# Cross-attention on one core: the rest of the context loaded in blocks and turned by VectorE, Wv turned into a tile of its own, and the last keys' products in 32-column tiles

## The chip, the cores and the metric

The kernel runs on one core of a Trainium2 chip. The metric is the device time in microseconds of one execution; before the change the median of three runs is 282.15 us (280.95 to 282.51). All arithmetic is in 32-bit floats.

## The reference

```
Q = x @ Wq                      # x: 16 x 256 x 256, 8 heads of 256
K = ctx @ Wk;  V = ctx @ Wv     # ctx: 16 x 77 x 192
score = Q K^T / sqrt(256)       # masked keys at -inf
attn  = softmax(score)
out   = (attn V) @ Wo + x
out   = layernorm(out) * gamma + beta
```

## The kernel before, in words

The kernel never forms Q, K and V. For each head h it forms G_h = Wk_h Wq_h^T (192 x 256), so that scores are x (G_h^T ctx^T), and U_h = Wv_h Wo_h (192 x 256), so that the output of a head is attn (ctx U_h). The 192 rows of G and U are kept as 128 (tiles gA, uA) and 64 (gB, uB); the context, transposed, likewise: cA holds the first 128 of its 192 features for all 16 x 77 keys, and cB the last 64, twice, in both halves of the partitions, so that products of depth 64 can run two at a time, one in each half of the rows of TensorE's array. Heads are worked in places: pair a holds heads a and a + 4.

The order on every engine is written out by hand: instructions run in each engine's queue in the order of the source, and waits between engines come from the tiles they share. PSUM has eight banks, all of one ring ("mm", pool `ps_mm`), so the ninth tile waits until the first has been copied out. SyncE issues every load, in the order of the source; load number n also waits until load n - 8 has landed.

The stages, in order:

- Loads: parts of Wk and Wq in rows, the first 336 keys of the context in rows (`load_c(0, first)`, tile c_sb, with `first` = 3 groups of 112 rows), the other halves of Wk and Wq in blocks of 32 rows (`load_blocks`), the other 896 keys (`load_c(first, NCR)`), Wv in blocks (16 loads of 96 KB), Wo (4 of 512 KB), the mask as integers into the tile bias, and x of the first four batches in blocks (`load_xT`, 4 loads of 256 KB in pieces of 256 bytes). Later, in the order of the source: x in rows, gamma, beta, then x of the next batches.
- TensorE turns the row-loaded weights and context by transposes (`turn_q`, `turn_k`, `turn_c`), VectorE turns the block-loaded ones 32 x 32 at a time (`turn_blk`, `turn_v`, `transpose_x`).
- `g_of`, `rest_of_g` and `of_pair` form G; `a_of_places` forms a = G^T ctx^T of the first four batches.
- `turn_c(first, NCR)` turns the rest of the context with TensorE (L653). The copies out of PSUM alternate between ScalarE and VectorE (`evacuate`), and GpSimd makes cB's second copy (L664), then cRA and cRB, the last 13 keys of each batch (L780, L781), zeroes vr (L782) and turns the integer mask into bias (L786).
- `of_pair` with Wv and Wo forms uA (tile pu, L676), `rest_of_pairs` forms uB (tile pw, L690), which GpSimd copies to the other half of the partitions (L805). GpSimd then forms differences of the blocks of uA and uB (part t2, L808 and L809), and adds to bias the not-a-number of a batch whose keys are all masked (L814).
- `prepare_last` forms vr, the values of the last 13 keys of all batches: eight PSUM tiles pr, each of 32 output columns for both halves e; `part_A` (L274) of depth 128 and `part_B` (L284) of depth 64. vr is laid out in blocks of 32 columns, of which 26 hold values; the other 6 are zeros. VectorE turns it during the loop (`turn_last`).
- The loop over 16 batches: scores (L313), softmax on VectorE (L328, L335, L348), ScalarE (L342) and GpSimd (L356), values of the next batch (pv, L241 and L252), a of the next four batches (pa, L199 and L213), attention times values (pm and po, L429; po, L378), the sum with x and the layer norm.

In the weights of `of_pair`, pgb reads contiguous columns of kT_blk, while pu reads every fourth column of wvT:

```python
def wv_part(a, e, n):
    return flat(wvT[half(e), a]).rearrange("p (l n) -> p n l", n=4)[:, n]
```

Of the kernel before, what the change touches and what calls it, by code (L numbers as in the profile page):

```python
# [8 lines left out]
F32 = mybir.dt.float32  # L9
I32 = mybir.dt.int32  # L10
AF = mybir.ActivationFunctionType
ALU = mybir.AluOpType
# [3 lines left out]
P = 128  # L16
H = 8
D = 256
EPS = 1e-05
GB = 4  # L20
KM = 64
# [32 lines left out]
def kernel(  # L54
# [15 lines left out]
    S2, DL = c.shape[1], c.shape[2]  # L70
    LB = DL - P
    CR = 112
    NCR = B * S2 // CR
    NG = B // GB
    QT = S // P
    NT = B * QT
# [5 lines left out]
    NL = DL // BK  # L82
    PW = (NF + 1) * BK
    assert KM == 2 * BK and NM == NF and 2 * KR <= BK
    assert NCR * CR == B * S2 and NG * GB == B and DI == 2 * P and D == 2 * P and 2 * LB == P


    engines = mybir.EngineType
# [25 lines left out]
    def of_e(u, e):  # L114
        return u[:, 3 - 2 * e : 5 - 2 * e].rearrange("p q n i c -> p (q n) i c")
# [3 lines left out]
    cB = const.tile([P, B, S2], F32, tag="cB", name="cB")  # L119
    cRA = const.tile([P, B, KR], F32, tag="cRA", name="cRA")  # L120
    cRB = const.tile([P, B, KR], F32, tag="cRB", name="cRB")
    vr = const.tile([P, B, DI], F32, tag="vr", name="vr")
    p_ring = [const.tile([P, NM, PW], F32, tag=f"p{i}", name=f"p_{i}") for i in range(2)]
    for p in p_ring:
        nc.gpsimd.memset(p[:, :, 2 * S2 :], 0.0)
# [10 lines left out]
    def flat(ap):  # L136
        return ap.rearrange("p a b -> p (a b)")

    def half(i):
        return slice(i * LB, (i + 1) * LB)  # L140
# [31 lines left out]
    def transpose_x(g, j):  # L172

        cols = xT_of[g][:, j * NM : (j + 2) * NM]
        nc.vector.transpose(cols, cols)
# [91 lines left out]
    def prepare_last():  # L267


        pr = [ps_mm.tile([P, 2, B, KR], F32, tag="mm", name=f"pr_{n}") for n in range(DI // BK)]  # L270

        def part_A(e):
            for n, o in enumerate(pr):
                nc.tensor.matmul(  # L274
                    o[:, e].rearrange("p b k -> p (b k)"),
                    flat(of_e(uA, e)[:, n]),
                    flat(cRA),
                    start=(e == 0),
                    stop=(e == 1),
                )  # L280

        def part_B(e):
            for n, o in enumerate(pr):
                nc.tensor.matmul(  # L284
                    o[:, e].rearrange("p b k -> p (b k)"),
                    flat(of_e(uB, e)[half(n % 2), n]),
                    flat(cRB[half(n % 2)]),
                    start=(e == 1),
                    stop=(e == 0),
                )  # L290

        part_A(0)
        part_B(0)
        part_B(1)
        part_A(1)
        for n, o in enumerate(pr):
            to = vr[:, :, n * BK : n * BK + 2 * KR]
            evacuate(to.rearrange("p b (e k) -> p e b k", e=2), o)
# [241 lines left out]
    early = ctx.enter_context(tc.tile_pool(name="early", bufs=1))  # L540
    pools[0] = turned = early
    with tc.tile_pool(name="wonce", bufs=1) as wp:
        c_sb = wp.tile([CR, NCR, DL], F32, tag="c", name="c_sb")


        wq_nat = wp.tile([P, 2, 2, 2 * D], F32, tag="w128", name="wq_nat")
# [13 lines left out]
            for i in range(NM):  # L560
                nc.sync.dma_start(to[i * BK : (i + 1) * BK], blocks[i])

        def load_c(lo, hi):
            nc.sync.dma_start(c_sb[:, lo:hi, :], c_rows[:, lo:hi, :])

        first = -(-GB * S2 // CR)
        nc.sync.dma_start(wk_nat[:, 0], wk_rows[0][:, : 2 * D])
        nc.sync.dma_start(wq_nat[:, 0], wq_rows[0][:, :, : 2 * D])
        nc.sync.dma_start(wk_nat[:, 1], wk_rows[1][:, : 2 * D])
        nc.sync.dma_start(wq_nat[:, 1], wq_rows[1][:, :, : 2 * D])  # L570
        nc.sync.dma_start(wk_last, wk_ends[:, : 2 * D])
        load_c(0, first)
        for e in range(2):
            load_blocks(wk_blk[:, e], wk_blocks[2 * e + 1])
            load_blocks(wq_blk[:, e], wq_blocks[2 * e + 1])
        load_c(first, NCR)

        warm = const.tile([P, 1], F32, tag="warm", name="warm")
        nc.scalar.activation(warm, eps, AF.Exp)
# [8 lines left out]
            load_blocks(wvT[:, a], wv_blocks[a])  # L588
        for a in range(NF):
            nc.sync.dma_start(wo_of[a // 2][:, a % 2], wo_rows[a])  # L590
        nc.sync.dma_start(
            bias_f.bitcast(I32), mask.rearrange("b k -> (b k)").partition_broadcast(P)
        )
# [24 lines left out]
        def turn_q(e, u):  # L618
            chunks = [
                wq_nat[:, e, t, u * D + dc * P : u * D + (dc + 1) * P]  # L620
                for dc in range(2) for t in range(2)
            ]
            pt = turn_chunks(chunks, f"q_{e}_{u}")
            evacuate(flat(qT[:, e, u]), flat(pt))

        def turn_k(e):
            pt = turn_chunks([wk_nat[:, e, n * P : (n + 1) * P] for n in range(4)], f"k_{e}")
            evacuate(
                kT[:, e].rearrange("p u n l -> p (u n) l")[:, :, :P], pt
            )  # L630
# [13 lines left out]
                    blk[:, e].rearrange("p m (n c) -> p m n c", c=BK),  # L644
                )

        def turn_c(lo, hi):
            for r in range(lo, hi, 2):
                n = min(2, hi - r)
                pc = ps_mm.tile([P, 4, P], F32, tag="mm", name=f"pc_{r}")  # L650
                for lc in range(2):
                    for j in range(n):
                        nc.tensor.transpose(  # L653
                            pc[:, 2 * lc + j, :CR],
                            c_sb[:, r + j, lc * LB : lc * LB + P],
                            ident[:CR, :CR],
                        )
                rows = slice(r * CR, (r + n) * CR)
                evacuate(flat(cA)[:, rows].rearrange("p (j m) -> p j m", m=CR), pc[:, :n, :CR])
                evacuate(  # L660
                    flat(cB)[LB:, rows].rearrange("p (j m) -> p j m", m=CR),
                    pc[LB:, 2 : 2 + n, :CR],
                )
                nc.gpsimd.tensor_copy(flat(cB)[:LB, rows], flat(cB)[LB:, rows])  # L664

        def turn_v(a):
            blocks = wvT[:, a].rearrange("p m (c n) -> p m n c", n=4)
            nc.vector.transpose(blocks, blocks)

        def of_pair(out, a, weight, moving):

            for n in range(4):
                for e in range(2):
                    nc.tensor.matmul(  # L676
                        out[e][:, a % 2, :],
                        weight(a, e, n)[:, :P],
                        moving(a, e, n),
                        start=(n == 0),  # L680
                        stop=(n == 3),
                    )
# [23 lines left out]
            return kT_blk[half(e), a, n]  # L706

        def wv_part(a, e, n):
            return flat(wvT[half(e), a]).rearrange("p (l n) -> p n l", n=4)[:, n]

        def wo_part(a, e, n):
            return wo_of[a // 2][half(e), a % 2, n, :]
# [1 line left out]
        def g_of(e):  # L714

            pg = ps_mm.tile([P, 2, DI], F32, tag="mm", name=f"pg_{e}")
            for u in range(2):
                for dc in range(2):
                    nc.tensor.matmul(
                        pg[:, u],  # L720
                        kT[:, e, u, dc, :P],
                        qT[:, e, u, dc],
                        start=(dc == 0),
                        stop=(dc == 1),
                    )
            nc.scalar.mul(gA[:, NF * e : NF * e + 2], pg, D ** -0.5)
# [23 lines left out]
        keep_busy(4)  # L750
        turn_q(0, 0)
        turn_q(0, 1)
        turn_k(1)
        g_of(0)
        turn_q(1, 0)
        turn_q(1, 1)
        turn_k_last()
        turn_c(0, first)
        g_of(1)
        rest_of_g(0)  # L760
        rest_of_g(1)
# [14 lines left out]
        nc.sync.dma_start(bet, beta.partition_broadcast(P))  # L776
        a_of_places((2, 3))
        turn_v(3)
        turn_c(first, NCR)
        nc.gpsimd.tensor_copy(cRA, cA[:, :, KM:])  # L780
        nc.gpsimd.tensor_copy(cRB, cB[:, :, KM:])  # L781
        nc.gpsimd.memset(vr, 0.0)  # L782

        nc.gpsimd.tensor_scalar(bias_f, bias_f.bitcast(I32), 0.0, -MASKED, ALU.is_equal, ALU.mult)  # L786

        for j in range(NF // 2):
            pu = two_banks("pu", j)
            for a in range(2 * j, 2 * j + 2):  # L790
                of_pair(pu, a, wv_part, wo_part)
            for e in range(2):
                evacuate(
                    of_e(uA, e)[:, :, 2 * j : 2 * j + 2].rearrange("p n a c -> p a n c"),
                    pu[e].rearrange("p a (n c) -> p a n c", c=BK),
                )
        for j in range(NF // 2):
            for e, pw in enumerate(
                rest_of_pairs(j, (2 * j, 2 * j + 1), wv_part, wo_part, "pw")
            ):  # L800
                for i, engine in enumerate((nc.scalar.copy, nc.vector.tensor_copy)):
                    a = 2 * j + i
                    here, there = (of_e(uB, e)[half(k), :, a] for k in (i, 1 - i))
                    engine(here, pw[half(i)].rearrange("p (n c) -> p n c", c=BK))
                    nc.gpsimd.tensor_copy(there, here)  # L805
        for u in (uA, uB):
            t2, _, b22, b11, b12 = (u[:, q].rearrange("p n i c -> p (n i c)") for q in range(5))
            nc.gpsimd.tensor_tensor(t2, b22, b12, ALU.subtract)  # L808
            nc.gpsimd.tensor_tensor(t2, t2, b11, ALU.add)  # L809
        nan = wp.tile([P, B, 1], F32, tag="nan", name="nan")  # L810
        nc.vector.tensor_reduce(nan[:, :, 0], bias, AX.X, ALU.max)
        nc.gpsimd.tensor_tensor(nan, nan, nan, ALU.mult)
        nc.gpsimd.tensor_tensor(nan, nan, nan, ALU.subtract)
        nc.gpsimd.tensor_tensor(bias, bias, nan.to_broadcast([P, B, S2]), ALU.add)  # L814

        for j in range(0, GT, 2):
            transpose_x(0, j)
        prepare_last()


# [126 lines left out]
```

## Time and profile before

| What | us |
|---|---|
| median of three runs | 282.15 (280.95 to 282.51) |
| the profiled execution | 280.93 |
| its span, first to last instruction | 279.2 |
| PE busy in the span | 269.7 (97%) |
| DVE, ACT, POOL busy | 206.0, 166.4, 168.2 |
| one round of the loop | 14.1 |

The page lists busy time of each engine, then the span in slices, then the chain of work that ended last, then groups of instructions by line. PE is TensorE's products, PEld its weight loads, DVE VectorE, ACT ScalarE, POOL GpSimd, SP SyncE, SPq its queue of DMA issues. A group names its line, engine, output and input tiles, shapes and count. Two instructions of the profile make one 32-bit product of TensorE, so the 8 products of one part_A appear as 16.

The granted TensorE clock is 0.993 over the span, and lower only at its end.

### The profile page before, as it was taken

To read this page: it belongs to the slowest core of one execution; us is meant where nothing else is said; L and a number is where in the kernel's file an instruction comes from. 1 tells how busy PE (TensorE), PEld (TensorE's weight loads), DVE (VectorE), ACT (ScalarE), POOL (GpSimd) and SP (SyncE) were. 2 spreads that over 40 slices of the span, in tenths; PEclk is the share of its full clock that TensorE was granted. 3 is DMA by queue.
4 is the path that set the end of the run, shared out by engine and by line. 5 is a ranking of instruction groups with operands and counts; after the bars stand their busy time and mean duration, and the time that the engine had idled before them with its cause. 6 is when DMAs were issued, how large, how long until landed. Compare 5 with 4: busy or idle time off the path is not lost.

```text
span 279.2 us, 13274 instructions
## 1 busy us (share of the span) xinstructions
PE 269.7 (97%) x5924; PEld 194.8 (70%) x5924; DVE 206.0 (74%) x421; ACT 166.4 (60%) x447; POOL 168.2 (60%) x228
## 2 busy tenths in 40 slices
PE   8899999999999999999999999999999999999990
PEld 7756599976495959595959585858686858476550
DVE  0353953777738989878788888787787878788873
ACT  2303222146738586868676767777776766978751
POOL 1000069947677777787877777777778445426183
PEclk9999999999999999999999999999999999999997
DMA  6997999920000101940100009501001011010112
GB/s 198 247 223 154 305 262 236 225 82 4 2 6 2 40 5 41 190 155 4 42 2 30 16 25 190 172 5 42 4 5 40 2 42 38 4 41 2 40 39 77
DMA packets 35641, 22.61 MB, mean 81 GB/s; under 512 B 17712, under 2 KB 34048, under 8 KB 35584
## 3 DMA queue, kind: packets, MB, share of 16 engines
q1 hardware_dynamic: 35584, 21.77, 31.1%
q8 instruction: 46, 0.75, 1.2%
q14 instruction: 11, 0.09, 0.1%
HBM read 17.57 MB, written 4.19 MB: 78 GB/s over the span
## 4 chain that ended last, share of the span: by engine, by line
PE 88%; DMA 3%; POOL 2%; ACT 2%; DVE 1%; SPq 1%; issue 0%; ACTq 0%; POOLq 0%
PE ps L313 23%; PE pa L199 12%; PE pv L241 9%; PE po L429 9%; PE pm L429 7%; PE pa L213 6%; PE pv L252 5%; PE po L378 5%; DMA c_sb<-in_ctx_dram 3%; PE pu L676 3%; PE pr L274 2%; ACT e L342 1%; PE pw L690 1%; PE pgb L676 1%; PE pr L284 1%; PE pc L653 1%
## 5 line engine op out<-in xcount | busy, mean ns | idle before, releaser
L342 ACT ACTIVATE e<-s,top 128x77 f32<-128x77 f32 x256 | 67.1, 346 | 52.1 <-DVE top L335 49.9
L356 POOL TENSOR_TENSOR p<-e,rden 128x512 f32<-128x512 f32 x64 | 45.9, 739 | 46.7 <-DVE rden L350 46.4
L313 PE MATMUL ps<-a,xT 128*32 128x154 f32 x2048 | 70.0, 294 | 0.0
L313 PEld LDWEIGHTS ps<-a,xT 128*32 128x32 f32 x2048 | 66.1, 110 | 1.7 <-issue 0.8
L328 DVE TENSOR_TENSOR s<-ps,bias 128x308 f32<-128x308 f32 x64 | 30.3, 474 | 17.7 <-PE ps L313 15.9
L199 PE MATMUL pa<-cA,gA 128*32 128x308 f32 x512 | 35.8, 423 | 0.0
L462 POOL TENSOR_TENSOR xg<-xg,m 128x256 f32<-128x256 f32 x33 | 24.2, 732 | 13.5 <-DVE xg L476 11.8
L199 PEld LDWEIGHTS pa<-cA,gA 128*32 128x32 f32 x512 | 16.4, 110 | 20.9 <-issue 8.0
L241 PE MATMUL pv<-uA,cA 128*32 128x512 f32 x256 | 30.4, 592 | 0.0
L366 DVE STREAM_TRANSPOSE pT<-p 128x640 f32<-128x640 f32 x32 | 25.6, 824 | 2.4 <-POOL p L356 2.4
L348 DVE TENSOR_REDUCE den<-e 128x8 f32<-128x616 f32 x32 | 24.7, 772 | 3.4 <-ACT e L342 3.4
L335 DVE TENSOR_REDUCE top<-s 128x8 f32<-128x616 f32 x32 | 25.5, 795 | 1.1
L664 POOL COPY cB<-cB 64x224 f32<-64x224 f32 (+1 forms) x6 | 1.9, 359 | 35.2 <-DVE cB L153 35.2
L392 POOL TENSOR_TENSOR ts<-vw 128x768 f32<-128x768 f32 x11 | 21.9, 1995 | 0.0
L213 PE MATMUL pa<-cB,gB 64*32 64x308 f32 x512 | 19.5, 420 | 0.0
L378 PE MATMUL po<-vw,pT 128*32 128x256 f32 x320 | 19.2, 380 | 0.0
L859 ACT COPY vw<-pv 128x512 f32<-128x512 f32 x32 | 16.9, 579 | 2.5 <-PE pv L252 2.5
L495 ACT ACT_TABLE_LOAD x14 | 18.0, 1283 | 0.3
L213 PEld LDWEIGHTS pa<-cB,gB 64*32 64x32 f32 x512 | 9.7, 107 | 11.3 <-issue 7.6
L252 PE MATMUL pv<-uB,cB 64*32 64x512 f32 x256 | 17.4, 601 | 0.0
L524 DVE SCALAR_TENSOR_TENSOR xg<-xg,mv,gam 128x256 f32<-128x256 f32 x25 | 17.1, 683 | 0.0
L378 PEld LDWEIGHTS po<-vw,pT 128*32 128x32 f32 x320 | 10.0, 110 | 9.5 <-DVE den L348 2.5
(114 smaller groups left out, 444.9 us busy)
## 6 DMA issues: line engine op xcount, KB each, us to landing
xT<-in_x_dram SPq DMA_DIRECT2D x16, 256.0 KB, 6.2
xg<-in_x_dram SPq DMA_DIRECT2D x4, 1024.0 KB, 7.9
out_dram<-xg SPq DMA_DIRECT2D x15, 256.0 KB, 2.3
wo<-in_L_xattn_Wo_dram SPq DMA_DIRECT2D x4, 512.0 KB, 6.2
wvT<-in_L_xattn_Wv_dram SPq DMA_DIRECT2D x16, 96.0 KB, 3.0
wq_nat<-in_L_xattn_Wq_dram SPq DMA_DIRECT2D x2, 512.0 KB, 5.9
wq_blk<-in_L_xattn_Wq_dram SPq DMA_DIRECT2D x8, 128.0 KB, 5.1
wk_blk<-in_L_xattn_Wk_dram SPq DMA_DIRECT2D x8, 96.0 KB, 5.6
```

Of the source, the lines that this page charges most:

```text
L199: nc.tensor.matmul(flat(o[i * BK : (i + 1) * BK]), gA[:, h, cols(dc, i)], flat(cA[:, batches, :]), start=not B_first, stop=B_first,)
L213: nc.tensor.matmul(flat(banks[j + k][i * BK : (i + 1) * BK]), gB[half(k), h % NF, cols(dc, i)], flat(cB[half(k), batches, :]), start=B_fir ...
L241: nc.tensor.matmul(pv[k][i * BK : (i + 1) * BK], cA[:, b, k * BK : (k + 1) * BK], uA[:, parts, :, i], start=True, stop=False,)
L252: nc.tensor.matmul(pv[k][i * BK : (i + 1) * BK], cB[half(k), b, k * BK : (k + 1) * BK], uB[half(k), parts, :, i], start=False, stop=True,)
L313: nc.tensor.matmul(ps[m // 2][i * BK : (i + 1) * BK, m % 2 * 2 * S2 : (m % 2 + 1) * 2 * S2], xT_of[g][:, j * NM + m, dc], flat(a_of[g][:, ...
L328: nc.vector.tensor_tensor(s[:, a * H // 2 : (a + 1) * H // 2], ps[a][:, : H // 2 * S2].rearrange("p (h k) -> p h k", k=S2), bias[:, b, :]. ...
L335: nc.vector.tensor_reduce(top, s, AX.X, ALU.max, negate=True)
L342: nc.scalar.activation(e[:, h], s[:, h], AF.Exp, bias=top[:, h : h + 1])
L356: nc.gpsimd.tensor_tensor(part, e_mh[:, :, :, keys], rden_mh.unsqueeze(3).to_broadcast(list(part.shape)), ALU.mult,)
L366: nc.vector.transpose(pT_of[t].rearrange("p n m q -> p m n q"), p.rearrange("p m (n k) -> p m n k", k=BK),)
L378: nc.tensor.matmul(po[i * BK : (i + 1) * BK], pT[:, n, i], vw_of[b][:, 2 - n // 2 * 2 : 4 - n // 2 * 2, n % 2, :] if n < NF else vr[:, b, ...
L429: nc.tensor.matmul(out[i * BK : (i + 1) * BK], weight[:, i], moving, start=(n == 0), stop=(n == len(terms) - 1),)
```

## The change

- The rest of the context no longer passes through c_sb and TensorE. After Wo, ahead of the mask, six DMAs (`load_rest`) write 32 x 32 blocks straight into cA and cB, in pieces of 128 bytes, 896 pieces each. VectorE turns them in place (`turn_rest`), and GpSimd copies cRA, cB's other half and cRB behind it. `turn_rest` stands after the products of the second half of pu and ahead of the copies of those products to uA.
- `g_of(0)` stands ahead of `turn_k(1)`, so that products of G come before the second transposes of Wk.
- `turn_v` writes to wv_turned, so that pu and pw read contiguous columns. wv_turned shares its buffer with vr, which is now allocated after pw; only the last 6 columns of every 32 of vr are zeroed, on VectorE.
- The mask is turned into bias on VectorE, after the copies to uA; bias gets its not-a-number ahead of the differences of uA and uB.
- The products of `prepare_last` write 32 output columns each, in four tiles of TensorE, instead of 128.

```diff
-            for n, o in enumerate(pr):
-                nc.tensor.matmul(
-                    o[:, e].rearrange("p b k -> p (b k)"),
-                    flat(of_e(uA, e)[:, n]),
-                    flat(cRA),
...
+                for i in range(NM):
+                    nc.tensor.matmul(
+                        o[i * BK : (i + 1) * BK, e].rearrange("p b k -> p (b k)"),
+                        of_e(uA, e)[:, n, i],
+                        flat(cRA),
...
+            for n in range(0, len(pr), 2):
+                for i in range(NM):
+                    for k in range(2):
+                        nc.tensor.matmul(
+                            pr[n + k][i * BK : (i + 1) * BK, e].rearrange("p b k -> p (b k)"),
+                            of_e(uB, e)[half(k), n + k, i],
+                            flat(cRB[half(k)]),
...
-        c_sb = wp.tile([CR, NCR, DL], F32, tag="c", name="c_sb")
+        first = -(-GB * S2 // CR)
+        c_sb = wp.tile([CR, first, DL], F32, tag="c", name="c_sb")
...
+        rest = slice(first * CR, None)
+        def load_rest():
+            blocks = c.rearrange("b k l -> (b k) l")[rest].rearrange("(m r) l -> r m l", r=BK)
+            for l in range(NL):
+                i, of = (l, cA) if l < NM else (l - NM + LB // BK, cB)
+                nc.sync.dma_start(
+                    flat(of)[i * BK : (i + 1) * BK, rest].rearrange("p (m q) -> p m q", q=BK),
+                    blocks[:, :, l * BK : (l + 1) * BK],
+                )
+
+        def turn_rest():
+            nc.vector.transpose(flat(cA)[:, rest], flat(cA)[:, rest])
+            nc.gpsimd.tensor_copy(cRA, cA[:, :, KM:])
+            nc.vector.transpose(flat(cB)[LB:, rest], flat(cB)[LB:, rest])
+            nc.gpsimd.tensor_copy(flat(cB)[:LB, rest], flat(cB)[LB:, rest])
+            nc.gpsimd.tensor_copy(cRB, cB[:, :, KM:])
...
-        load_c(first, NCR)
...
         for a in range(NF):
             nc.sync.dma_start(wo_of[a // 2][:, a % 2], wo_rows[a])
+        load_rest()
         nc.sync.dma_start(
             bias_f.bitcast(I32), mask.rearrange("b k -> (b k)").partition_broadcast(P)
         )
...
+        wv_turned = const.tile([P, NF, 4, DL], F32, tag="vr", name="wv_turned")
+
         def turn_v(a):
-            blocks = wvT[:, a].rearrange("p m (c n) -> p m n c", n=4)
-            nc.vector.transpose(blocks, blocks)
+            nc.vector.transpose(
+                wv_turned[:, a].rearrange("p n (m r) -> p m n r", r=BK),
+                wvT[:, a].rearrange("p m (c n) -> p m n c", n=4),
+            )
...
         def wv_part(a, e, n):
-            return flat(wvT[half(e), a]).rearrange("p (l n) -> p n l", n=4)[:, n]
+            return wv_turned[half(e), a, n]
...
         turn_q(0, 1)
+        g_of(0)
         turn_k(1)
-        g_of(0)
...
-        turn_c(first, NCR)
-        nc.gpsimd.tensor_copy(cRA, cA[:, :, KM:])
-        nc.gpsimd.tensor_copy(cRB, cB[:, :, KM:])
-        nc.gpsimd.memset(vr, 0.0)
...
-        nc.gpsimd.tensor_scalar(bias_f, bias_f.bitcast(I32), 0.0, -MASKED, ALU.is_equal, ALU.mult)
...
             for a in range(2 * j, 2 * j + 2):
                 of_pair(pu, a, wv_part, wo_part)
+            if j:
+                turn_rest()
             for e in range(2):
                 evacuate(
...
+        nc.vector.tensor_scalar(bias_f, bias_f.bitcast(I32), 0.0, -MASKED, ALU.is_equal, ALU.mult)
...
+        vr = const.tile([P, B, DI], F32, tag="vr", name="vr")
+        ends = flat(vr).rearrange("p (n c) -> p n c", c=BK)[:, :, 2 * KR :]
+        nc.vector.memset(ends, 0.0)
         prepare_last()
```

The order of the two blocks after the copies of uB is also exchanged: the not-a-number of bias (L811 to L814) now stands ahead of the differences t2 (L808, L809).

More of the change, by code (lines that the diff above doesn't have):

```diff
@@ L72 @@
     CR = 112
-    NCR = B * S2 // CR
     NG = B // GB
@@ L84 @@
     assert KM == 2 * BK and NM == NF and 2 * KR <= BK
-    assert NCR * CR == B * S2 and NG * GB == B and DI == 2 * P and D == 2 * P and 2 * LB == P
+    assert NG * GB == B and DI == 2 * P and D == 2 * P and 2 * LB == P
     engines = mybir.EngineType
@@ L121 @@
     cRB = const.tile([P, B, KR], F32, tag="cRB", name="cRB")
-    vr = const.tile([P, B, DI], F32, tag="vr", name="vr")
     p_ring = [const.tile([P, NM, PW], F32, tag=f"p{i}", name=f"p_{i}") for i in range(2)]
@@ L273, in part_A @@
             for n, o in enumerate(pr):
-                nc.tensor.matmul(
-                    o[:, e].rearrange("p b k -> p (b k)"),
-                    flat(of_e(uA, e)[:, n]),
-                    flat(cRA),
-                    start=(e == 0),
-                    stop=(e == 1),
-                )
-        def part_B(e):
-            for n, o in enumerate(pr):
[L284 to L290, printed above, removed]
+                for i in range(NM):
[3 more added lines that the diff above has]
+                        flat(cRA),
+                        start=(e == 0),
+                        stop=(e == 1),
+                    )
+        def part_B(e):
+            for n in range(0, len(pr), 2):
[5 more added lines that the diff above has]
+                            flat(cRB[half(k)]),
+                            start=(e == 1),
+                            stop=(e == 0),
+                        )
         part_A(0)
@@ L561, in load_blocks @@
                 nc.sync.dma_start(to[i * BK : (i + 1) * BK], blocks[i])
-        def load_c(lo, hi):
-            nc.sync.dma_start(c_sb[:, lo:hi, :], c_rows[:, lo:hi, :])
-        first = -(-GB * S2 // CR)
+        rest = slice(first * CR, None)
+        assert (B * S2 - first * CR) % BK == 0
+        def load_rest():
[5 more added lines that the diff above has]
+                    blocks[:, :, l * BK : (l + 1) * BK],
+                )
+        def turn_rest():
[4 more added lines that the diff above has]
+            nc.gpsimd.tensor_copy(cRB, cB[:, :, KM:])
         nc.sync.dma_start(wk_nat[:, 0], wk_rows[0][:, : 2 * D])
@@ L571 @@
         nc.sync.dma_start(wk_last, wk_ends[:, : 2 * D])
-        load_c(0, first)
+        nc.sync.dma_start(c_sb, c_rows[:, :first, :])
         for e in range(2):
@@ L645, in turn_blk, with turn_c @@
                 )
-        def turn_c(lo, hi):
-            for r in range(lo, hi, 2):
-                n = min(2, hi - r)
+        def turn_c():
+            for r in range(0, first, 2):
+                n = min(2, first - r)
                 pc = ps_mm.tile([P, 4, P], F32, tag="mm", name=f"pc_{r}")
@@ L664, in turn_c @@
                 nc.gpsimd.tensor_copy(flat(cB)[:LB, rows], flat(cB)[LB:, rows])
+        wv_turned = const.tile([P, NF, 4, DL], F32, tag="vr", name="wv_turned")
         def turn_v(a):
-            blocks = wvT[:, a].rearrange("p m (c n) -> p m n c", n=4)
-            nc.vector.transpose(blocks, blocks)
+            nc.vector.transpose(
+                wv_turned[:, a].rearrange("p n (m r) -> p m n r", r=BK),
+                wvT[:, a].rearrange("p m (c n) -> p m n c", n=4),
+            )
         def of_pair(out, a, weight, moving):
@@ L757 @@
         turn_k_last()
-        turn_c(0, first)
+        turn_c()
         g_of(1)
@@ L805 @@
                     nc.gpsimd.tensor_copy(there, here)
[L806 to L809, printed above, removed]
         nan = wp.tile([P, B, 1], F32, tag="nan", name="nan")
@@ L814 @@
         nc.gpsimd.tensor_tensor(bias, bias, nan.to_broadcast([P, B, S2]), ALU.add)
+        for u in (uA, uB):
+            t2, _, b22, b11, b12 = (u[:, q].rearrange("p n i c -> p (n i c)") for q in range(5))
+            nc.gpsimd.tensor_tensor(t2, b22, b12, ALU.subtract)
+            nc.gpsimd.tensor_tensor(t2, t2, b11, ALU.add)
         for j in range(0, GT, 2):
             transpose_x(0, j)
+        vr = const.tile([P, B, DI], F32, tag="vr", name="vr")
+        ends = flat(vr).rearrange("p (n c) -> p n c", c=BK)[:, :, 2 * KR :]
+        nc.vector.memset(ends, 0.0)
         prepare_last()
```

## The prediction

> **What bounds the kernel now.** I read the page first: span 279.2 us, PE busy 97%, nine tenths or more of every slice but the first few and the last. Then the chain of waits in order of time over the stretch that the change touches (columns: start us, length us, what):
>
> ```profile
> 34.51 1.68 PE pc L653 x16
> 36.19 7.77 PE pu L676 x64
> 43.96 3.68 PE pw L690 x64
> 47.64 3.01 PE pr L274 x16
> 50.65 3.02 PE pr L284 x32
> 53.66 3.01 PE pr L274 x16
> 56.67 4.33 PE ps L313 x128
> ```
>
> No idle piece stands between them, and none does from 11.51 us to 258 us: TensorE alone sets the time here. So a TensorE instruction that goes is a gain of its length, as long as nothing that feeds the next one comes late; everything on the other engines is worth only its lateness. Who is near to late? The timeline of GpSimd (start, length):
>
> ```profile
> 39.14 3.50 POOL L782 MEMSET vr<- 128x4096 f32 x1
> 42.74 4.38 POOL L786 TENSOR_SCALAR bias<-bias 128x1232 f32<-128x1232 int32 x1
> 47.19 3.57 POOL L805 COPY uB<-uB 64x256 f32<-64x256 f32 x8
> ```
>
> The eight uB copies end at 50.76 while L284, which reads uB, begins at 50.65: GpSimd is already level with TensorE, so taking TensorE time out ahead of it gives nothing unless GpSimd gets room too. Last, SyncE's queue, which issues every load:
>
> ```profile
> 15.90 0.45 SPq L564 DMA_DIRECT2D c_sb<-in_ctx_dram  x1
> 16.39 12.46 SPq L561 DMA_DIRECT2D wvT<-in_L_xattn_Wv_dram  x16
> 28.90 1.86 SPq L590 DMA_DIRECT2D wo<-in_L_xattn_Wo_dram  x4
> 30.81 0.70 SPq L591 DMA_DIRECT2D bias<-in_mask_BxS_if_dram  x1
> 31.56 9.55 SPq L168 DMA_DIRECT2D xT<-in_x_dram  x4
> ```
>
> Sixteen issues take 12.46 us because each load waits for the one eight places earlier (the instruction order shows eight semaphores in turn), and one waited 2.9 us for c_sb, landed at 15.90 + 8.2 = 24.1. The DMA share is near or above 1.0 in most 4 us windows to 56 us, so landings follow one another. By issue plus time to landing: the last wo 38.2, bias 40.5, the four xT from 41.4 to 46.2.
>
> **What the Trainium skill says.** "TensorEngine Tiling (Array Packing)", Key Properties: changing the tiling mode drains TensorE. The trace agrees: scores after the 128x128 products take 4.33 us, after 128x32 products (L429) 4.19. "TensorE: Matmul & The Clock Gate", LDWEIGHTS: a load's time goes by its columns, P/1.2 ns. By that 27 ns for 32 columns and 107 for 128; the trace has 110 and 187, so the direction agrees and the sizes don't, and it shows what the page leaves out: 326 ns for 128 strided columns (pu). "DMA: Bandwidth & Descriptors", Why small descriptors are slow: about three cycles of overhead a packet, so a 256-byte one costs 11. By that, 128 bytes cost 7: an estimate, since no run here shows 128-byte packets.
>
> **The change, part by part.**
>
> *1. Rest of the context.* The 16 instructions of L653 for the rest go: 1.68 us of TensorE. With them go 4 ScalarE copies, 4 VectorE copies and 4 GpSimd copies; none is on the chain.
>
> *2. Wv in its own tile.* The weights of pu are now contiguous, as those of pgb in the same form are already. pgb has 32 instructions in 3.65 us, 114 ns each; pu 64 in 7.77, 121. At pgb's pace pu takes 64 x 114 = 7.30; but pgb includes a 0.1 us start once. Spacing from pair to pair is about 216 ns in pgb, 233 in pu: 32 pairs x 17 = 0.56, and the first pair's longer start 0.1. I take 0.65, bounds 0 (if the spacing isn't the stride's doing) and 0.75. pw has 57.5 ns each against phb's 59: nothing. The transposes L668 (1.65 us, strided both sides) should fall towards the 0.95 us of the same size in L642; VectorE hides them.
>
> *3. 32-column tiles.* Passes of 208 columns follow at 176 ns in pr; 308 columns in four tiles follow at 259 (L199). Both are columns/1.2 + 2.5 ns, so the products themselves gain nothing though their instructions go from 64 to 192. What differs is each start: the first load of 128 columns holds up a pass by about 0.1 us, that of 32 by 0.03, three times; and scores then follow in the same mode, 4.33 - 4.19 = 0.14. In all 0.25; bounds -0.4 (should 4 small loads a group not hide) and 0.4.
>
> *4. G 0 ahead of turn_k(1).* TensorE waits 0.67 us at 7.63 for Wk's second half; pg fills some of it, but L653 at 11.51 then waits for c_sb, which lands at 11.47 as before. Nothing; not below, as pg's inputs are there by 7.6.
>
> *5. GpSimd and VectorE.* GpSimd loses the vr memset (3.50), the mask (4.38) and four 0.37 copies, gains one 64x896 copy (about 0.9 by the 224- and 256-element rows). VectorE gains two transposes of 896 columns (between 0.82 for 640 and 1.20 for 1024: 1.07 each), the mask (as its 1232-element reduction, 1.44) and a small memset of 768 strided elements (0.5; bounds 0.1 and 0.9). On GpSimd the NaN check of bias (two small pieces and the 2.25 us of L814) moves ahead of the u differences: with the uB copies done at about 48.6, uA's t2 (L808, L809) is there at 54, and pv reads it at 58.2, when the first scores end.
>
> *6. Loads: the risk.* SyncE issues six c loads (896 packets of 128 bytes each) after wo, ahead of mask, xT, x, gamma and beta. Working it out: without c_sb's slot, Wv's ninth load waits for its first (about 21.4, not 24.1), so wo starts some 3.5 us sooner and ends at 34.7. The c loads have 5376 packets. xT moved 4096 in 46.2 - 40.5 = 5.7 us, 718 a us: 7.5 us at that pace, 4.8 if 7/11 holds. I take 6.5: last c at 41.2 (39.5 to 42.2), mask +2.4 = 43.6, xT +5.7 = 49.3.
>
> Behind them VectorE runs: transposes of cA and cB (waiting for the c loads), then uA (L151), the mask (waiting for it), four uB copies, the NaN reduction, xT (2.48 us), the memset of vr, the vr copies. TensorE would end pu at 41.6, pw at 45.3, part_A at 48.2. part_B(0) needs uB for all four pairs of e = 0: mask landing + 1.4 (mask) + 0.43 (a uB copy) + 5 x 0.45 (GpSimd) = landing + 4.1. So the mask may land at 44.1 at the latest; I have 43.6. Likewise xT: landing + 2.5 + 0.6 (memset, 0.5, with its semaphore) + 0.55 (ScalarE's vr copy frees the bank) must reach 54.0, when the scores could begin: at the latest 50.3; I have 49.3. The cover is thin, half a us and one.
>
> Sum: 1.68 + 0.65 + 0.25 = 2.6 us, less 0.1 for a small wait: 2.5. The profiled execution took 280.93 (span 279.2 and 1.7 around it), so it would give 278.4. It lies 1.2 below the median of the runs shown, 282.15; the forecast goes by the median: 279.6.
>
> **Rivals.**
>
> *The loads come late and take half* (0.20). At 625 packets a us (160 GB/s of 256-byte packets in the window 40 to 42) c takes 8.6, the mask lands at 45.7, and part_B waits 1.6: gain 1.0, 281.2. For it: landings in the trace are irregular, and one xT issue stood 3.9 us. Against it: half the bytes a packet.
>
> *Slower: VectorE blocked in turn_rest* (0.12). If 128-byte packets are worth only 400 a us, c takes 13.4 and lands at 48.1, mask 50.5, 6.4 after its latest: 282.15 - 2.6 + 6.4 = 286. It decides from 9.6 us for the six loads (560 packets a us): the mask then lands at 46.7, and the wait of 2.6 eats the whole gain. For it: all of VectorE's evacuations, and so the PSUM banks and uB, stand behind that wait. Against it: 256-byte packets do better than that in every window but the worst.
>
> *The change gives only its first part* (0.10): the spacing of pu isn't the stride's, or the small tiles cost what they save: 1.0 to 1.7, 280.7.
>
> **How the numbers follow.** Mine has 0.58. A measurement can tell 0.5%, 1.4 us, from no change. Faster by more: nearly all of mine (0.56), 0.06 of the late loads, 0.05 of the last, 0.67. Within: 0.02, 0.12, 0.05 and 0.01 of the blocked one: 0.20. Slower: 0.13. Range: down to 277.8 (parts at their upper bounds, 3.2, and 1.2 for where the median of few runs falls), up to 282.6, which takes in the late loads and the start of the slower case.
>
> **What would show it.** In the chain after: pc x16 gone, pu 7.1 us, the three pr pieces 2.9 to 3.0 each, ps 4.2, pw's end near 45.3 and scores from 54.0, then the same pieces to the end. A gap before pr L285, or pieces of DVE, POOL or DMA c in the chain between 41 and 54, is the late-load case. A gap ahead of pu, or a scores stage that isn't 2.6 us sooner with no gap, would make the prediction wrong in its sums; so would a loop longer than its 14.1 us a round.

## The result, and the profile after

The change makes no difference that can be measured. The median goes from 281.88 us (280.88 to 283.34, 20 runs) to 281.84 us (280.27 to 284.27, 20 runs); the ratio is 1.0004, with a 95% interval from 0.9982 to 1.0025. The forecast was 279.6, 0.8% faster.

The profiled execution took 281.82 us, its span 280.0, 0.8 more than before. The chain of waits in order of time shows where (start us, length us, what):

```profile
35.06 7.11 PE pu L700 x64
42.17 3.61 PE pw L714 x64
45.78 2.95 PE pr L273 x64
48.73 2.97 PE pr L285 x128
51.71 0.48 PE pr L273 x7
52.19 1.84 issue
54.03 2.78 PE pr L273 x57
56.81 2.23 PE ps L314 x68
59.04 0.63 issue
59.67 2.15 PE ps L314 x58
61.82 1.85 PE pv L239 x14
```

The piece of L653 is gone and pu takes 7.11, as forecast. But two pieces of "issue" stand in TensorE's stream: the engine stood still and waited for nothing that the profile names, 1.84 us in the middle of the last part_A and 0.63 in the scores. Before, no such piece stood there. The time from pw's end to the end of the first pv is 17.89 us against 15.07: the first two parts and pw gained 2.4 us, and this stretch loses 2.8, so 0.4 is lost.

Another 0.56 us comes from further ahead: c_sb landed at 12.03 instead of 11.47, and everything behind it shifted. (What follows the first pv takes 0.2 less.) Over the twelve profiled executions of this study that landing lies anywhere from 11.44 to 13.03. The loads ahead of it are the same in all of them, so I take it for scatter; no run tests that.

The waits that the prediction feared did not come. The timeline of VectorE and GpSimd:

```profile
43.60 0.80 DVE L817 TENSOR_SCALAR bias<-bias 128x1232 f32<-128x1232 int32 x1 [0.67 <-DMA bias<-in_mask_BxS_if_dram]
...
44.60 3.60 POOL L826 COPY uB<-uB 64x256 f32<-64x256 f32 x8 [1.49 <-ACT uB L825]
...
49.70 2.49 DVE L173 STREAM_TRANSPOSE xT<-xT 128x512 f32<-128x512 f32 x4 [1.24 <-DMA xT<-in_x_dram]
```

The mask and xT are each waited for, 0.67 and 1.24 us, on VectorE; uB is complete at 48.20, before L285 wants it at 48.73. The gap at 52.19 stands in part_A, which reads none of the three (it reads uA and cRA), so it isn't theirs. In the page's table of queues, q8 has grown with the program; first before, then after (packets, MB, share of the DMA engines' time):

```profile
q8 instruction: 46, 0.75, 1.2%
```

```profile
q8 instruction: 48, 0.79, 1.2%
```

### The profile page after: what moved, and what is told of

Same layout as the page of the kernel before. It is cut to its first block, busy times and chain, and to the rows that moved or that the text cites. A ratio compares the mean times of both kernels' runs of the same rounds, so it can differ in the third digit from the quotient of the medians.

```text
span 280.0 us, 13622 instructions
## 1 busy us (share of the span) xinstructions
PE 268.3 (96%) x6100; PEld 191.0 (68%) x6100; DVE 208.7 (75%) x421; ACT 165.3 (59%) x443; POOL 160.4 (57%) x223
## 4 chain that ended last, share of the span: by engine, by line
PE 87%; DMA 3%; POOL 2%; ACT 2%; DVE 1%; issue 1%; SPq 1%; ACTq 0%; POOLq 0%
PE ps L314 23%; PE pa L197 12%; PE pv L239 9%; PE po L430 9%; PE pm L430 7%; PE pa L211 6%; PE pv L250 5%; PE po L379 5%; DMA c_sb<-in_ctx_dram 3%; PE pu L700 3%; PE pr L273 2%; ACT e L343 1%; PE pgb L700 1%; PE pw L714 1%; PE pr L285 1%
## 5 line engine op out<-in xcount | busy, mean ns | idle before, releaser
L357 POOL TENSOR_TENSOR p<-e,rden 128x512 f32<-128x512 f32 x64 | 45.9, 739 | 49.6 <-DVE rden L351 40.5
L197 PEld LDWEIGHTS pa<-cA,gA 128*32 128x32 f32 x512 | 17.9, 110 | 19.4 <-issue 6.8
L883 ACT COPY a<-pa 128x308 f32<-128x308 f32 x48 | 16.6, 446 | 0.0
```

The source lines that it names most:

```text
L197: nc.tensor.matmul(flat(o[i * BK : (i + 1) * BK]), gA[:, h, cols(dc, i)], flat(cA[:, batches, :]), start=not B_first, stop=B_first,)
L357: nc.gpsimd.tensor_tensor(part, e_mh[:, :, :, keys], rden_mh.unsqueeze(3).to_broadcast(list(part.shape)), ALU.mult,)
L883: nc.scalar.copy(dst, src)
```

## The experiments

**Theory 1:** TensorE ran out of instructions. They come to it by DMA in blocks (queue q8, 16 KB packets). Before, TensorE has 11894 instructions in the trace (products, weight loads and some forty for semaphores) and 46 such packets; after, 12241 and 48: 259 and 255 instructions a packet. And the two gaps stand 256 instructions apart, ahead of numbers 1474 and 1730 of TensorE's stream, counted in order of start. So a block is 256 instructions, and I call the place between two blocks an edge. The small tiles turn the 9 us of pr from 128 such instructions into 512, and a block that must come every few us comes late while the DMA queues are full of loads. All the traces of this study bear out the count: they have twelve such pieces of over 0.3 us between 12 us and the kernel's end, in eight different kernels, and each stands ahead of number 194 plus a multiple of 256.

**Rival A:** a wait for VectorE or GpSimd that the trace doesn't name. **Rival B:** small tiles are slower of themselves.

### e1_wide: the wide products back, all else as changed

```diff
-                for i in range(NM):
-                    nc.tensor.matmul(o[i * BK : (i + 1) * BK, e]..., of_e(uA, e)[:, n, i], flat(cRA), ...)
+                nc.tensor.matmul(o[:, e]..., flat(of_e(uA, e)[:, n]), flat(cRA), ...)
```

and part_B likewise.

> The changed kernel with the products of the last keys again 128 columns wide, as before the change. Theory 1 (TensorE runs out of fetched instructions: in the small tiles it uses up 256 instructions in about 3.3 us, while a block of instructions comes by DMA and queues behind the loads): the gap of 1.84 us inside pr goes, the gap of 0.63 in the scores goes or shrinks, the three pr pieces take 9.0 us in all, and the kernel is 2.0 us faster than the changed one, 0.7% faster than before. Rival A (the gap is a wait on another engine that the trace doesn't name, VectorE's memset or GpSimd's copies): the gap stays within 0.3 us, and the time is that of the changed kernel, within 0.3%.

Measured: ratio to before 0.9923 (0.9900 to 0.9946), median 279.41. The chain:

```profile
45.42 3.01 PE pr L272 x16
48.43 3.02 PE pr L282 x32
51.44 3.01 PE pr L272 x16
54.45 4.32 PE ps L311 x128
```

No gap. Without its third part the change gains 0.77%, 2.2 us of 281.5 (1.5 to 2.8), where the first two parts were to give 2.3. Rival A falls: memset, mask and c loads stand where the change put them.

### e2_narrow_only: the small tiles alone, on the kernel before

The diff is the first two hunks of the change's.

> The kernel before with only the products of the last keys in 32-column tiles. Theory 1: a gap of 1 to 2 us without a named wait stands inside pr or in the first scores, at a count of TensorE instructions that lies a multiple of 256 from the next such gap, and the time is 0.3 to 0.8% above before. Rival A: no gap, since the memset, the mask and the c loads are where they were; 0.25 us faster than before, not to be told from it.

Measured: 1.0046 (1.0025 to 1.0066), slower. Its trace has one gap, in the scores:

```profile
57.37 1.81 PE ps L316 x50
59.18 0.88 issue
60.07 2.69 PE ps L316 x75
```

It stands ahead of number 1730 alone; pr comes 2.4 us later here than in the changed kernel, and no block was late inside it. part_B takes 3.25 us instead of 2.97, 0.3 of it a wait for the uB copies, which GpSimd made at 47.8 to 51.4. So the small tiles alone cost 0.46%, 1.3 us. The gap is smaller than the 1 to 2 us expected, the time as expected.

### e3_late_loads and e4_wide_late: the next batches' loads one round later

```diff
-            if n == 0:
+            if n == (g == 1):
                 load_xT(g)
                 load_x(g)
```

on the changed kernel (e3) and on e1_wide (e4).

> The changed kernel, with the loads of x for batches 4 to 7 (xT and xg, 2 MB) issued one round of the loop later, so that fewer loads stand in the DMA queues between 49 and 63 us. Theory 1: the fetch at about 51.5 finds shorter queues; the gap at 52 to 54 shrinks (by 0.5 to 1.5, for x of the first batches and gamma and beta are still on the queues then), the one at 59 goes; 0.4 to 0.9% faster than the changed kernel. Rival A: as the changed kernel within 0.3%. Rival B (the small tiles are simply slower there, whatever the DMA does): also as the changed kernel.

> Both: 128-column products and the later loads of x. Theory 1: no gap left, as the 128-column products alone (within 0.2%), 0.7 to 0.9% faster than before. Rival A: as the changed kernel.

Measured: e3 0.9984 (0.9967 to 1.0002), e4 0.9936 (0.9911 to 0.9960). The gaps of e3 stand before the same instructions and are shorter, 1.04 and 0.35 us (1.84 and 0.63 in the changed kernel); a third, of 0.34, stands at 179 us. That is less than expected, because the edit did little: SyncE waits for nothing at that place, and the issue of xT moved only from 49.0 to 51.9 us. The direction agrees with theory 1, but with this run alone it would stay open; a stronger edit follows. e4 is as e1 within its interval; it has no gap in pr or the first scores, but one of 0.58 us at 121.75, ahead of number 4546.

### e5_quiet: the loads held back

```diff
-        load_x(0)
-        nc.sync.dma_start(gam, ...); nc.sync.dma_start(bet, ...)
...
         for t in new:
             shift(t)
+        if b < 0:
+            xg_of[0] = const.tile([P, GT, DI], F32, tag="xg0", name="xg_0")
+            nc.vector.memset(xg_of[0][:, :, :1], 0.0)
+            nc.sync.dma_start(xg_of[0], x_rows[:, :GT, :])
+            nc.sync.dma_start(gam, ...); nc.sync.dma_start(bet, ...)
```

> The changed kernel, small tiles kept, with x in rows, gamma, beta and the next batches' x held back: a VectorE memset of one column of xg behind the first scores' shift makes SyncE wait until about 61 us, so that the DMA queues are empty from about 50 us on. Theory 1 (the fetch of instructions queues behind loads): both gaps go, for the same instructions in the same order come with empty queues; pr then takes 8.9, scores follow at once, and the kernel is as the one with wide products or up to 0.2 us better: 0.7 to 0.9% faster than before. Rival B (small tiles make TensorE stop whatever the DMA does): the gaps stay within 0.3 us, the time as the changed kernel's. A loss of its own would be new gaps at 62 to 75, where the held loads now run.

Measured: 0.9996 (0.9975 to 1.0016). The time missed the expectation, and the chain tells why:

```profile
51.55 2.95 PE pr L273 x64
54.50 4.19 PE ps L314 x128
...
64.53 3.52 PE ps L314 x100
68.06 2.47 issue
70.53 0.58 PE ps L314 x9
```

Both gaps are gone (the first two pieces of pr take 2.95 and 2.98), with the same instructions in the same order. A new one of 2.47 us stands in the second scores, where the held loads now run. The windows (us; busy of PE, PEld, DVE, ACT, POOL with counts; granted clock; DMA share, which is the time that packets took as a share of 16 engines' time; GB/s) show the two sides. First the changed kernel, then e5_quiet:

```profile
52.00:56.00 4.00, 2.16 (x54) 1.43 (x51) 2.00 (x4) 1.23 (x3) 3.84 (x4) 1.00 1.11 184
```

```profile
52.00:56.00 4.00, 4.00 (x112) 3.36 (x104) 2.80 (x6) 2.12 (x4) 3.84 (x4) 1.00 0.00 0
...
68.00:72.00 4.00, 1.53 (x36) 1.29 (x38) 0.71 (x3) 2.18 (x8) 1.68 (x3) 1.00 1.05 166
```

In these windows TensorE stands still where the DMA share is above 1, and not where it is 0, and the gap goes along with the loads. Rival B falls: with empty queues the small tiles run at full pace. The blocks by the trace (number of the TensorE instruction at the block's edge, when it was reached, when the next q8 packet began, when TensorE went on at the following edge):

| kernel | edge | reached | next packet, its length | following edge passed |
|---|---|---|---|---|
| changed | 1218 | 48.70 | 51.50, 0.88 | 54.03, after the gap |
| changed | 1474 | 54.03 | 56.53, 1.30 | 59.67, after the gap |
| e5_quiet | 1474 | 51.69 | 51.89, 0.96 | 56.43, no gap |
| e5_quiet | 1986 | 63.29 | 67.87, 1.27 | 70.53, after the gap |

With empty queues the packet begins 0.2 us after TensorE has entered the block before; in the rows with full ones 2.5 to 4.6 us after. In these gaps TensorE goes on 1.4 to 1.8 us after the packet's end. The twelve traces agree: they have one packet for each edge, but for one at the end of e8_shift, and TensorE nowhere passes an edge sooner than 1.26 us after its packet's end. The fastest block took 3.1 us (e5_quiet, in pr). So 0.2 + 1.0 + 1.6 = 2.8 us just keep up, and 2.8 + 0.9 + 1.6 = 5.3 don't.

Full queues don't always delay a packet. In the changed kernel TensorE passes an edge at 115.55, where the DMA share from 115 to 116 us is 1.42, and the packet begins 0.2 us later.

### e6_half: tiles of 64 columns

```diff
+        HC = 2 * BK
...
+                for i in range(2):
+                    nc.tensor.matmul(o[i * HC : (i + 1) * HC, e]..., two(uA, e, n, i), flat(cRA), ...)
```

`two` takes 64 of the 128 columns; part_B likewise.

> The changed kernel with tiles of 64 columns in the products of the last keys: 128 instructions of matrix work where the wide form has 64 and the small tiles 256, for the same columns. Theory 1: 256 instructions then last about 9 us, not 3.3, and no gap stands in pr (at most 0.3 us in the scores); pr takes 8.9 to 9.0 us; 0.7 to 0.9% faster than before, as the wide form. Rival B: half of the loss of the small tiles, 1.2 us of gaps, 0.4% faster than before.

Measured: 0.9915 (0.9895 to 0.9935), median 279.31: no gap in pr or in the loop but one of 0.35 us at 177 us, pr pieces of 2.96, 2.97 and 2.96. Half as many instructions is few enough, and the cost isn't in proportion to the tiles: it sets in where a block is used up sooner than one comes. It was near, though: the packet that follows edge 1218 began 3.4 us after TensorE had passed it and ended at 55.01, and TensorE passed the next edge at 56.66, 1.65 us later, within the 1.3 to 1.8 us that it takes in the gaps. In the profiled execution there was next to nothing to spare. This version and e1_wide beat both kernels; e6_half lies 0.1 us ahead of e1_wide, which can't be told apart.

### e7_mask_pool: the mask on GpSimd again

```diff
-        nc.vector.tensor_scalar(bias_f, bias_f.bitcast(I32), 0.0, -MASKED, ALU.is_equal, ALU.mult)
+        nc.gpsimd.tensor_scalar(bias_f, bias_f.bitcast(I32), 0.0, -MASKED, ALU.is_equal, ALU.mult)
```

on e1_wide.

> The changed kernel with wide products (the first experiment), and the mask turned into bias on GpSimd again, in the new order, ahead of the uB copies. By the prediction's step on GpSimd: mask landed at 42.3 to 43.6, 4.4 us on GpSimd to 47.3, then the eight uB copies to 50.9, where TensorE wants the first five by 48.4: a gap of 1 to 2 us ahead of the depth-64 products, waiting for GpSimd, and the kernel 0.3 to 0.7% slower than with wide products alone. Rival (GpSimd has room, the move of the mask was worth nothing): within 0.2% of wide products alone, no gap.

Measured: 0.9992 (0.9973 to 1.0011), 0.7% behind e1_wide. The chain runs through GpSimd:

```profile
44.04 4.39 POOL bias L814
...
50.76 0.41 POOL uB L823
51.21 4.61 PE pr L282 x32
```

TensorE waits 2.2 us for the uB copies ahead of the depth-64 products, and then L282 takes 4.61 us instead of 3.02: the granted clock was 0.50 for 3.4 us from 52.6 on, in this execution. So in the new order the gain hangs on the mask's move to VectorE: without it 0.08% is left, within the noise.

### e8_shift: 16 instructions fewer at the start

```diff
-        keep_busy(14)
+        keep_busy(6)
```

> The changed kernel with 8 idle transposes fewer at the very start, which TensorE spends before its first load has landed: 16 instructions fewer ahead of pr. Theory 1 with blocks of 256 instructions: the gaps keep their place in the stream's blocks, so that each falls 8 products later in the source: after 15 products of the last part_A instead of 7, and after 76 of the scores instead of 68. Rival A or any wait for data: the gaps stay before the same products, 7 and 68. The time is that of the changed kernel.

Measured, the ratio from a few runs: 1.0023 (1.0006 to 1.0040). The gap moved:

```profile
51.99 0.83 PE pr L273 x14
52.82 2.43 issue
55.25 3.88 PE pr L273 x49
```

It stands after 14 products, not after 7, and again ahead of number 1474 of the stream. (15 products were expected; the trace has 15 TensorE instructions fewer, not 16, one for a semaphore having come in.) Nothing that these products read or write has moved by 7 products; the place is the block's edge. The second gap didn't come: the packet after the edge began 1.5 us behind it, not 2.5. What came instead is in the windows (the columns as before):

```profile
55.00:57.00 2.00, 1.75 (x23) 1.25 (x25) 0.59 (x1) 0.17 (x1) 1.81 (x2) 0.50 1.03 221
```

From 54.80 on, 2.0 us into the gap, the granted clock was at half for 3.4 us, and passes of 208 columns followed at 347 ns instead of 176: the 49 products behind the gap took 3.88 us, 1.6 more than at the full clock. So a late block can cost more than its wait.

### e9_spread: small tiles, loads spread out

e5_quiet, and the next batches' xT held by the same kind of memset to the round after (issued at 72.6 us), their xg to the one after that (88.0).

> The changed kernel with its small tiles, and the loads spread: x in rows, gamma and beta held until 61 us as before, x of batches 4 to 7 in blocks held by the same means to the next round of the loop (about 71 us), in rows to the one after (about 85 us), so that no stretch of loads after 50 us lasts longer than 6 us. Theory 1: the instruction fetch finds its turn in time everywhere, no gap over 0.5 us is left, and the small tiles cost nothing: as 64-column tiles within 0.2%, 0.8 to 1.0% faster than before. Rival: a loss of the small tiles of their own, 0.3% or more slower than 64-column tiles; or a gap at 71 to 77 with the new load, 1 us and more.

Measured: 0.9996 (0.9976 to 1.0015); missed. No gap in pr or the first scores, but two smaller ones where the loads now stood:

```profile
65.03 3.53 PE ps L314 x100
68.56 0.62 issue
...
78.14 1.95 PE po L430 x68
80.10 1.07 issue
```

They are 1.7 us together. Loads of 6 us are long enough to make a block late, since the loop uses up a block in 3.5 to 7 us all the way. But loads in the loop needn't cost anything: every version loads the x of its last eight batches there, and in the changed kernel, with a DMA share of 0.94 to 1.23 between 112 and 120 us, no gap stands beside them. In e3, e4 and e6 one of 0.34 to 0.58 us does. So whether a load in the loop makes a block late depends on where it meets an edge. The wide products of pr, with 128 TensorE instructions in 9 us, were the safer place.

### e10_wv_only: Wv's tile alone, on the kernel before

```diff
+        wv_turned = [wp.tile([P, 2, 4, DL], F32, tag=t, name=f"wv_{t}") for t in ("wqb", "wkb")]
```

with `turn_v` and `wv_part` as in the change.

> The kernel before with Wv alone turned into tiles of its own (two tiles in the buffers of wq_blk and wk_blk), all else as before. By the prediction, GpSimd is level with TensorE there: pu goes from 7.77 to 7.1, then TensorE waits some 0.5 us for GpSimd's uB copies ahead of the depth-64 products, and nothing is gained: within 0.1% of before. Rival (GpSimd follows sooner too): 0.6 us, 0.2% faster.

Measured: 0.9969 (0.9954 to 0.9984), and the rival was right:

```profile
36.16 7.11 PE pu L680 x64
...
49.89 3.06 PE pr L284 x32
```

The whole gain of pu arrives; L284 loses 0.04. GpSimd's copies still end at 50.72, but L284 needs only the first five at its start, as the prediction itself counted further down, and the others arrive while it runs.

## Why the prediction was wrong

The step that failed is part 3, the small tiles: "In all 0.25; bounds -0.4 (should 4 small loads a group not hide) and 0.4". It counted their instructions, even too few (192 products' where the profile has 64 + 128 + 64 = 256, for 64 before), and asked only whether the array hides them, not whether they arrive in time; that term it put at nothing without a reason. The array does hide them: in e5_quiet, undisturbed, the three pr pieces and the scores take 13.07 us against 13.37 before, a gain of 0.30, as worked out. In the changed kernel the same stretch takes 16.03, a loss of 2.66, because two blocks of instructions came late. No rival had this. The first two made TensorE wait for data; the third, in which "the small tiles cost what they save", came nearest in its place, but named no cause. That 281.84 lies inside the range, which went up to 282.6, is luck: it went so far for data that comes late, and none did.

The other steps, one by one:

- *Part 1:* L653 is gone from the chain, 1.68 us. Right.
- *Part 2:* pu 7.11 against 7.1 forecast; weight loads of 187 ns instead of 326 in the trace. e10_wv_only shows it to be the layout of Wv's tile, as nothing else was changed there: 0.31% (0.16 to 0.46) for a forecast 0.23%. The transposes L689 still take 1.56 to 1.64 us each and didn't fall to 0.95; they are hidden.
- *Part 4:* nothing, right. pg runs earlier, and L672 still waits for c_sb.
- *Part 5:* transposes 1.10 and 1.11 (1.07 forecast), cB copy 0.93 (0.9), memset 0.70 (0.5), mask 0.80 (1.44, too high). That time taken out ahead of GpSimd gives nothing was wrong: in e10_wv_only 0.7 us came through. But the direction holds: with the mask left on GpSimd in the new order, 2.2 us are lost (e7_mask_pool).
- *Part 6:* wo landed at 35.4 (34.7 forecast), the last c at 39.8 (41.2), the mask at 43.6 (43.6), xT at 49.6 (49.3). The mask took 3.8 us behind c, not 2.4, and c landed 4.4 behind wo, not 6.5: two misses that cancel, so the 43.6 was luck. The 4.4 us aren't the time of the c packets: in the trace they run from 33.3, 2.1 us before wo has landed, to 39.3, so 5376 packets took 6.0 us, 900 a us, partly beside others. Nor were 718 a us the pace of the 256-byte packets: in the kernel before, those of xT start at 37.3, ahead of the mask's landing at 40.5. The better measure is the packet itself: 18 ns in the mean for 128 bytes in the changed kernel, 25 for 256 bytes in the kernel before. That ratio, 0.71, is near the 7/11 = 0.64 of the estimate from the Trainium skill's page "DMA: Bandwidth & Descriptors" (Why small descriptors are slow). No rival of late loads came true.

The sum of parts 1 and 2, 2.3 us, lies close to the 2.2 that e1_wide measured.

What stays open is which part of a late block is queueing behind data packets, and which is the fetch's own time: the trace shows when a packet starts and ends, not when it was asked for. Nor is it shown why full queues delay one packet by 4.6 us and another by 0.2.

## What to carry to other kernels

Count a change's instructions on the bounding engine and the time in which they run, and lay that beside the loads that run at the same moment: here 256 TensorE instructions in less than about 5 us beside full DMA queues can make TensorE stop. Gaps of "issue" in an engine's stream that always stand a multiple of the same number of instructions apart point to late blocks of program, not to missing data, as all twelve did here. Put heavy loads beside stages of few, long instructions, and prefer wide products there: splitting 128 columns into four tiles saved 0.3 us at best and cost 2.7 where the loads ran, while 64-column tiles kept the gain, if by a narrow margin.

## What the runs showed of the hardware that I had not expected

- Instructions of TensorE come in blocks of 256 (16 KB). With idle DMA queues the packet of a block starts 0.2 us after TensorE enters the block before (e5_quiet). At the twelve gaps it started 2.1 to 4.6 us after, and TensorE went on 1.3 to 1.8 us after its end.
- The granted clock fell to 0.50 for 3.4 us in two traces: 1.4 us after a wait of 2.2 us in e7_mask_pool, and 2.0 us into a gap of 2.4 us in e8_shift. At gaps of 1.8 us and less, and at one of 2.5 us in e5_quiet, it stayed at 1.00, so the length of the gap alone doesn't decide it.
- A packet of 128 bytes took 18 ns in the mean (changed kernel), one of 256 bytes 25 (kernel before).
- Weight loads of 128 columns took 326 ns with a stride of four elements and 187 contiguous; pairs of passes of 256 columns followed every 233 ns with the former and every 216 with the latter.
- The mask of 1232 elements took 4.38 us on GpSimd and 0.80 on VectorE.
